# The fifth part of an output projection takes another quarter of x, some sums move earlier, one input load moves later

## The chip, the cores and the metric

The kernel runs on one core of a Trainium2 chip. The metric is the device time of one execution in microseconds (us), lower is better, as the median of several executions. Engines are named as in the profile: PE (matrix multiply), PEld (its weight load), DVE (vector), ACT (activations), POOL (GpSimd), SP (which here only issues transfers).

## What is computed

Eight images of 512 channels by 32x32 pixels (a matrix of 512 by 1024) each go through two attention layers with different weights. In each layer

```python
xn  = group_norm(x, 8 groups) * gamma + beta
q, k, v = wq @ xn + bq, wk @ xn + bk, wv @ xn + bv      # 512 x 1024 each, 8 heads of 64
att = softmax(q_head.T @ k_head / 8)                    # 1024 x 1024 for each head
x   = x + wp @ (att @ v_head for all heads) + bp
```

All numbers are 32-bit floats. The output is x after the second layer.

## The kernel before

**Jobs.** An image in a layer is a job. Images go in pairs, so jobs 0 to 3 are image 0 in layer 0, image 1 in layer 0, image 0 in layer 1, image 1 in layer 1, then the next pair. Image 0 stays in one tile x of 128 partitions by 4 chunks by 1024 columns through jobs 0 and 2.

**One pass of the main loop (variable n)** runs the attention of job n, then the V product of job n+1, and then three projections product by product: O, the output projection of job n, and K and Q of job n+1. The profile shows this as stages: an attention of 110 us and then a stretch of projections of 88 to 94 us.

**Projections by seven products.** Each 512x512 by 512x1024 projection is done by Strassen's scheme in Winograd's form, with 7 half-size products in place of 8, and each of the seven is again done with 7 products of quarter size. The outer seven are called parts here and run in the order `OUTER = (1, 2, 6, 5, 7, 3, 4)`. A part is computed by a chain of seven PE steps (`chain`), in the order 1, 5, 6, 2, 7, 3, 4. The chain's result goes into a tile p of [128, 2, 512] out of the pool `epool`. Chains overlap: step j of chain c stands at place 7c+2j in PE's order, so a step of one chain alternates with a step of the next. After step 7 of a chain DVE reads the PSUM bank that step 4 of the same chain adds to again (`put(1, 1, z)` and then `product(4)` into z). Step 4 therefore waits for DVE.

**How a part reaches x.** `end(c)` runs in program order after the last step of chain c. For the output projection it calls `more(oh, sh, part, moved)`: part is to be added to the quarter (oh, sh) of x, where oh is the half of the channels and sh the half of the columns. With `moved` the sum is made by an accumulating transfer that POOL issues at once (L682). Without it an addition on DVE (L684) goes into the list `outer`, from which `thunk` takes one entry after each step 7 and each step 3 of later chains, and only when the list `soon` is empty. `soon` first holds four sums of the next job's xn and then four sums for the later output chains. The first entry of `outer` is so taken out at chain index 4, after `end(3)`, which is that of part 5. Quarter (0, 0) gets parts 1 and 2, quarter (0, 1) gets 6, 5 and 3, quarter (1, 1) gets 5 and 7, and quarter (1, 0) gets 7 and 4. Part 6 and part 7 are first combined on DVE with parts 1 and 6 (L668).

**DVE and ACT in attention.** For each of 64 steps PE makes a block of scores (L870), ACT its exponentials e (L875), DVE adds e to a running sum (L885 for the first two blocks of a group, L887 for the others) and PE multiplies e by v (L901). e comes from a pool of 6 buffers. After 8 steps `finish` reduces the sum (L917) and takes the product out of PSUM (L924). Between the steps a table of chores places other work at chosen steps. In pass 0 these are factors of weights (L154 to L160), the norm of job 1, the sums of xn for job 1 (`sums`, L385 to L391) and the sums of those sums (`deep_steps`, L423 to L429).

**Orders.** The orders of PE, ACT and DVE are the order in which the code calls them. SP's and POOL's orders come from the layer that builds the program, which also puts in the waits: an instruction that touches the same bytes as an earlier one waits for it. `later(delay, fn)` calls fn once a clock of the program's own, counted in assumed microseconds, has gone that far.

**Input of image 1.** `load_x(1)` issues four transfers of 512 KB on SP during the first projections (L219), into a tile that before held the raw Q weights. ACT reads it at steps 3 to 6 of the first attention.

Of the kernel before, what the change touches and what calls it, by code (L numbers as in the profile page):

```python
# [72 lines left out]
def fast_path(  # L73
# [34 lines left out]
    def later(delay, fn):  # L108
        todo.append((clock[0] + delay, fn))
# [96 lines left out]
    def used(key):  # L206
        del held[key]
        later(2.5, fetch)
# [8 lines left out]
    def load_x(b):  # L217
        for cc in range(NC):
            nc.sync.dma_start(xs[b][:, cc, :], x[b, cc * P : (cc + 1) * P, :])  # L219

    class Norm:
# [20 lines left out]
        def sums(self, cc):  # L242

            nc.scalar.activation(
                xn[0][:, cc, :], xs[self.b][:, cc, :], AF.Identity, accum_out=self.mv[:, cc, 0:1]
            )
# [327 lines left out]
    def deep_phases(n, extra, outs=None, early=()):  # L574
# [8 lines left out]
        def job(which):  # L583
            return n - 1 if which == O else n
# [74 lines left out]
        def end(c):  # L659
            which, o = chains[c]  # L660
            m = job(which)
            used((m, which, o))

            def p(k):
                return tiles[which, k]

            def add(to_, a, b):
                outer.append(lambda: nc.vector.tensor_add(to_, a, b))  # L668

            if which == O:  # L670
                b, layer = jobs[m]
                xt = xs[b]

                def more(oh, sh, part, moved=False):


                    cols = slice(sh * HALF, (sh + 1) * HALF)
                    to_ = xt[:, 2 * oh : 2 * oh + 2, cols]

                    def go():  # L680
                        if moved:
                            nc.gpsimd.dma_start(to_, p(part), accum_op=ALU.add)  # L682
                        else:
                            nc.vector.tensor_add(to_, to_, p(part))  # L684
                        parts[oh, sh] -= 1
                        if layer == 1 and parts[oh, sh] == 0:
                            rows = slice(oh * CH, (oh + 1) * CH)
                            later(8.0 if moved else 2.0, lambda: nc.sync.dma_start(
                                out[b, rows, cols].rearrange("(c p) s -> p c s", p=P), to_
                            ))  # L690

                    if moved:
                        go()
                    else:
                        outer.append(go)

                if o == 1:
                    more(0, 0, 1, True)
                elif o == 2:
                    more(0, 0, 2, True)  # L700
                elif o == 6:
                    add(p(6), p(6), p(1))
                    more(0, 1, 6)
                elif o == 5:
                    more(0, 1, 5)
                    more(1, 1, 5, m in (0, 2))
                elif o == 7:
                    add(p(7), p(7), p(6))
                    more(1, 0, 7)
                    more(1, 1, 7)  # L710
                elif o == 3:
                    more(0, 1, 3, True)
                elif o == 4:
                    more(1, 0, 4, True)
                return
            d = dst[which]

            def quarter(oh, sh):
                return d[:, 2 * oh : 2 * oh + 2, sh * HALF : (sh + 1) * HALF]

            if o == 2:
                add(quarter(0, 0), p(1), p(2))
            elif o == 6:
                add(p(6), p(6), p(1))
            elif o == 5:
                add(quarter(0, 1), p(6), p(5))
            elif o == 7:
                add(p(7), p(7), p(6))
                add(quarter(1, 1), p(7), p(5))
            elif o == 3:  # L730
                add(quarter(0, 1), quarter(0, 1), p(3))
            elif o == 4:
                add(quarter(1, 0), p(7), p(4))
# [28 lines left out]
        at = sorted((7 * c + 2 * j, c, j) for c in range(len(chains)) for j in range(7))  # L762
        at = [(c, j) for _, c, j in at]
# [6 lines left out]
    def last_weights(n):  # L770
        w = acts.tile([P, NW, 2, CH], F32, tag="deep", name="w_last")
        nc.sync.dma_start(w, factors[O, jobs[n][1]])
        return w
# [10 lines left out]
    def last_sums(sh):  # L784


        def start():
            if sh == 0:
                tx[0] = acts.tile([P, 3, 2, HALF], F32, tag="t", name="t_last")
            nc.vector.tensor_sub(last_right(sh, 5), last_right(sh, 7), last_right(sh, 1))  # L790

        def second():
            nc.vector.tensor_sub(last_right(sh, 6), last_right(sh, 3), last_right(sh, 5))

        def third():
            nc.vector.tensor_sub(last_right(sh, 7), last_right(sh, 3), last_right(sh, 7))

        def fourth():
            nc.vector.tensor_sub(last_right(sh, 4), last_right(sh, 2), last_right(sh, 6))

        return start, second, third, fourth
# [258 lines left out]
    def extend_plan(n):  # L1060
        plan.extend((n, V, o) for o in ORDER)
        plan.extend((n - 1, O, o) for o in ORDER)
        plan.extend((n, which, o) for which in (K, Q) for o in OUTER)
# [212 lines left out]
    for n in range(-1, len(jobs)):  # L1276
        last = n + 1 == len(jobs)
        outs = None
        if n >= 0:
            chores = {}  # L1280

            def put(i, fn):
                while i in chores:
                    i += 1
                chores[i] = fn

            if last:
                w = last_weights(n)
                for i, fn in enumerate(last_sums(0)):
                    put(44 + 3 * i, fn)  # L1290
            else:
                if n == 0:
                    first_factors(put, [(O, 0), (V, 1)])
                elif n == 1:
                    first_factors(put, [(K, 1), (Q, 1)])
                elif n == 2:
                    first_factors(put, [(O, 1)])
                for i, (_, fn) in enumerate(extra):
                    put(2 + i, fn)
                at = (10, 19, 22, 24, 26, 28, 36, 39, 42, 45)  # L1300
                if n == 0:
                    for i, fn in zip((3, 3, 4, 5, 6, 8, 10, 11, 12, 13, 15), reads):
                        put(i, fn)
                    at = (22, 30, 34, 35, 37, 38, 41, 44, 47, 50)
                for i, fn in zip(at, steps + sums(n + 1)):
                    put(i, fn)
                deep_first = deep_steps(n + 1)
                for at, fn in zip((52, 54, 57, 59), deep_first[4:]):
                    put(at, fn)
                put(61, lambda: (extend_plan(n + 1), [fetch() for _ in range(RING)]))  # L1310
            assert max(chores, default=0) < NT * len(att.groups)
            att.run(chores)
            banks(0, "one")
            banks(1, "one")
            if last:
                for i, fn in enumerate(last_sums(1)):
                    later(4.1 + 1.5 * i, fn)
                later(9.9, judge)
                for sh in range(2):
                    last_proj(n, w, sh)  # L1320
                break
            outs = OutputSums(n)
            out_sums(n, outs)
            first = v_phase(n + 1, ORDER)
            for thunk in first[:-1]:
                thunk()
            rest = first[-1:]
            extra = deque()
            if jobs[n][1] == 1 and jobs[n][0] + 2 < B:
                extra.append((11, lambda b=jobs[n][0] + 2: (x_tile(b), load_x(b))))  # L1330
            if n == 1:
                load, bias_steps = make_out_bias(1)
                extra.append((8, load))
                extra.extend((11, fn) for fn in bias_steps)
            if n + 2 < len(jobs):
                reads, steps = norm_steps(n + 2)
                extra.extend((15, fn) for fn in reads)
        both = deep_phases(n + 1, extra, outs, deep_first[:4] if outs else ())
        both[0]()
        rest[0]()  # L1340
        if n < 0:
            later(22.0, lambda: load_x(1))
        for thunk in both[1:]:
            thunk()
        banks(0, "two")
        att = Attention(n + 1)
        att.scores(0)
        att.scores(1)
        banks(1, "two")
        att.scores(2, "po")  # L1350
# [249 lines left out]
```

## Time and profile before

| what | value |
|---|---|
| median of three executions | 3208.58 us (3206.6 to 3208.76) |
| the profiled execution's own time | 3205.31 us |
| its span, first to last instruction | 3203.5 us |
| PE busy | 3184.0 us, 99% of the span |
| DVE busy | 2773.0 us, 87% |
| ACT busy | 1913.1 us, 60% |
| POOL busy | 100.7 us, 3% |
| share of 16 DMA engines, SP's and POOL's transfers | 26.5% and 6.2% |

A line of the timeline gives the start in us from the span's beginning, the duration, the engine, the line of the code, the operation, the tile written and those read, how many instructions were merged, and in brackets the engine's idle time before it and what ended it. The chain of waits is the path that ended last, followed back from the end. Times of single instructions are from the profiled execution.

### The profile page before, as it was taken

The numbers are of one execution on the slowest core, as the hardware profiler recorded it, in microseconds if no ns is written. First come the engines' busy times: TensorE is split into PE (matmuls) and PEld (weight loads), VectorE is DVE, ScalarE is ACT, GpSimd is POOL, SyncE is SP. The second block draws the span as 40 slices with busy tenths as digits, with TensorE's granted clock in tenths as the row PEclk, the third lists the DMA queues.
The fourth block names the chain that finished last, engine by engine and source line by source line (L and its number), as shares of the span: only waits on it lengthen the run. The fifth ranks groups of instructions, "written<-read, shape, count | busy, mean of one in ns | idle before, by whom it ended". The sixth has DMA issues, their size and how long they took to land.

```text
span 3203.5 us, 57787 instructions
## 1 busy us (share of the span) xinstructions
PE 3184.0 (99%) x22917; PEld 1861.8 (58%) x22917; DVE 2773.0 (87%) x3989; ACT 1913.1 (60%) x3063; POOL 100.7 (3%) x95
## 2 busy tenths in 40 slices
PE   9999999999999999999999999999999999999999
PEld 7366384663836648366483754837547375573844
DVE  8897999979889798897988889888898888988877
ACT  4746646466565665656656565565656656566564
POOL 0000000000000000000000000000000000000000
PEclk9999999999999999999999999999999999999999
DMA  8234172350703315033160421505216051150511
GB/s 291 74 108 126 49 215 69 94 167 22 213 25 91 88 28 159 21 105 130 30 210 16 119 67 38 147 16 142 96 44 194 16 141 44 51 135 20 170 37 42
DMA packets 156998, 308.32 MB, mean 96 GB/s; under 512 B 34104, under 2 KB 60592, under 8 KB 156464
## 3 DMA queue, kind: packets, MB, share of 16 engines
q1 hardware_dynamic: 139856, 272.05, 26.5%
q0 software_dynamic: 16864, 32.51, 6.2%
q8 instruction: 181, 2.97, 0.4%
q14 instruction: 97, 0.79, 0.1%
HBM read 225.13 MB, written 45.68 MB: 85 GB/s over the span
## 4 chain that ended last, share of the span: by engine, by line
PE 95%; DVE 4%; DMA 0%; issue 0%; POOL 0%; ACT 0%; DVEq 0%; POOLq 0%
PE sc L870 27%; PE po L901 27%; PE zd L636 10%; PE vd L636 10%; PE z L494 6%; PE yd L636 5%; PE ud L636 4%; PE y L494 2%; PE v L494 2%; PE u L494 2%; DVE acc L887 0%; DMA x<-p 0%; PE z_last L814 0%; DVE w L156 0%; DVE p L655 0%
## 5 line engine op out<-in xcount | busy, mean ns | idle before, releaser
L875 ACT ACTIVATE e<-sc 128x1024 f32<-128x1024 f32 x1024 | 1044.3, 1024 | 564.2 <-PE sc L870 458.7
L870 PE MATMUL sc<-q,k 64*64 64x512 f32 x8192 | 1058.2, 589 | 0.0
L901 PE MATMUL po<-e,v 64*64 64x512 f32 x8192 | 1057.3, 589 | 0.0
L887 DVE TENSOR_TENSOR acc<-acc,e 128x1024 f32<-128x1024 f32 x768 | 936.4, 1219 | 58.7 <-ACT e L875 12.0
L901 PEld LDWEIGHTS po<-e,v 64*64 64x64 f32 x8192 | 313.2, 133 | 565.7 <-issue 553.3
L870 PEld LDWEIGHTS sc<-q,k 64*64 64x64 f32 x8192 | 311.5, 133 | 562.4 <-issue 544.8
L885 DVE TENSOR_TENSOR acc<-e,e 128x1024 f32<-128x1024 f32 x128 | 156.4, 1222 | 112.2 <-ACT e L875 112.1
L636 PE MATMUL zd<-deep,w 128*128 128x256 f32 x860 | 241.1, 380 | 2.7 <-DVE p L653 2.1
L636 PE MATMUL vd<-deep,w 128*128 128x256 f32 x804 | 224.3, 380 | 1.4 <-DVE p L655 1.3
L636 PEld LDWEIGHTS zd<-deep,w 128*128 128x128 f32 x860 | 162.8, 190 | 27.2 <-DVE p L653 3.4
L636 PEld LDWEIGHTS vd<-deep,w 128*128 128x128 f32 x804 | 152.3, 190 | 23.9 <-DVE p L655 2.5
L917 DVE TRANSPOSE_TENSOR_REDUCE r<-acc 128x32 f32<-128x1024 f32 x128 | 158.5, 1238 | 0.6
L682 POOL DMA_DIRECT2D x<-p x62 | 74.6, 1211 | 1971.4 <-ACT p L646 1525.1
L636 PE MATMUL vd<-os,w 128*128 128x256 f32 x420 | 118.1, 380 | 1.6 <-DVE p L655 1.6
L668 DVE TENSOR_TENSOR p<-p,p 128x1024 f32<-128x1024 f32 x94 | 114.2, 1215 | 0.0
L494 PE MATMUL z<-w,t 128*128 128x256 f32 x480 | 110.9, 379 | 0.0
L494 PE MATMUL z<-w,xn 128*128 128x256 f32 x480 | 110.1, 382 | 0.0
L518 ACT COPY v<-z 128x512 f32<-128x512 f32 x32 | 18.7, 585 | 148.7 <-PE z L494 148.7
L494 PEld LDWEIGHTS z<-w,xn 128*128 128x128 f32 x480 | 90.0, 190 | 23.8 <-issue 12.2
L442 ACT COPY ud<-zd 128x256 f32<-128x256 f32 x156 | 55.7, 357 | 76.6 <-PE zd L636 75.7
L653 DVE TENSOR_TENSOR p<-vd,s 128x256 f32<-128x256 f32 x63 | 26.7, 424 | 85.1 <-PE vd L636 85.1
L657 ACT COPY s<-vd 128x256 f32<-128x256 f32 x156 | 58.0, 372 | 69.7 <-PE vd L636 69.7
(242 smaller groups left out, 4192.6 us busy)
## 6 DMA issues: line engine op xcount, KB each, us to landing
w<-deep SPq DMA_DIRECT2D x287, 448.0 KB, 3.8
x<-p POOLq DMA_DIRECT2D x62, 512.0 KB, 6.6
rb<-rd SPq DMA_DIRECT2D x96, 256.0 KB, 4.0
w<-keep SPq DMA_DIRECT2D x84, 256.0 KB, 2.7
deep<-w SPq DMA_DIRECT2D x42, 448.0 KB, 3.7
w<-wqkv_dram SPq DMA_DIRECT2D x57, 256.0 KB, 2.8
x<-x_dram SPq DMA_DIRECT2D x28, 512.0 KB, 6.4
out_dram<-x SPq DMA_DIRECT2D x28, 512.0 KB, 6.4
```

Of the source, the lines that this page charges most:

```text
L442: nc.scalar.copy(u, z)
L494: nc.tensor.matmul(ps[:, ti * CH : (ti + 1) * CH], right(src, tx[0], o)[:, cc, t0 : t0 + P], w[:, cc, :], start=(start and ti == 0 and cc ...
L636: nc.tensor.matmul(ps, lhs[:, FACTOR[i], :], moving[i], start=start, stop=True, skip_group_check=True,)
L657: return chain(product, lambda ps: nc.scalar.copy(s5, ps), put, z, y, u, w)
L668: outer.append(lambda: nc.vector.tensor_add(to_, a, b))
L682: nc.gpsimd.dma_start(to_, p(part), accum_op=ALU.add)
L870: nc.tensor.matmul(sc[h * HD : (h + 1) * HD, j, :], k[r, hp, k0 : k0 + HD], q[r, hp, sh * HALF : (sh + 1) * HALF], start=True, stop=True,)
L875: nc.scalar.activation(e, sc, AF.Exp, scale=SCALE)
L885: nc.vector.tensor_add(acc[g], self.es[i - 1], e)
L887: nc.vector.tensor_add(acc[g], acc[g], e)
L901: nc.tensor.matmul(po[g][j * HD : (j + 1) * HD, h, :], v[r, kc, d0 : d0 + HD], e[r, j, :], start=(kc == 0), stop=(kc == NT - 1),)
L917: nc.vector.tensor_reduce(self.r[:, 0, m, :], self.acc.pop(g).rearrange("p j (b e) -> p (j b) e", e=RP), AX.X, ALU.add, apply_transpose=True,)
```

## The change

There are three edits.

1. In the output projections of jobs 0 and 2, the accumulating transfer of part 5 goes to quarter (0, 1), and the addition of part 5 to quarter (1, 1) is now DVE's. Before it was the other way round. In other jobs DVE makes both, before and after.
2. In the first attention (n = 0) the last chores are placed at earlier steps: the four sums of xn at 39, 41, 43, 45 (before 41, 44, 47, 50) and the last four of `deep_steps` at 47, 49, 51, 53 (before 52, 54, 57, 59). The two applications of the norm that were asked for at steps 37 and 38 are asked for at 36 and 37. Since step 35 is taken and a taken step passes a chore on to the next, all four stand where they stood.
3. `load_x(1)` is due 32 of the program's own microseconds after the first projections begin, before 22. In SP's order the first two of the four transfers stay where they were. The third now comes after the fetch of the last Q weights and one store of weight factors, and the fourth after two stores more.

```diff
@@ deep_phases, end(c)
+                fresh = m in (0, 2)
                 if o == 1:
                     more(0, 0, 1, True)
 ...
                 elif o == 5:
-                    more(0, 1, 5)
-                    more(1, 1, 5, m in (0, 2))
+                    more(0, 1, 5, fresh)
+                    more(1, 1, 5)
@@ chores of the attention
                 if n == 0:
 ...
-                    at = (22, 30, 34, 35, 37, 38, 41, 44, 47, 50)
+                    at = (22, 30, 34, 35, 36, 37, 39, 41, 43, 45)
                 for i, fn in zip(at, steps + sums(n + 1)):
                     put(i, fn)
                 deep_first = deep_steps(n + 1)
-                for at, fn in zip((52, 54, 57, 59), deep_first[4:]):
+                for at, fn in zip((47, 49, 51, 53) if n == 0 else (52, 54, 57, 59), deep_first[4:]):
                     put(at, fn)
@@ first projections
         if n < 0:
-            later(22.0, lambda: load_x(1))
+            later(32.0, lambda: load_x(1))
```

## The prediction, made before the changed kernel ran

> **What bounds the kernel now.** I read the page's busy shares first, then PE's waits stage by stage, then DVE, POOL and PE around the waits.
>
> ```profile
> span 3203.5 us, 57787 instructions
> PE 3184.0 (99%) x22917; PEld 1861.8 (58%) x22917; DVE 2773.0 (87%) x3989; ACT 1913.1 (60%) x3063; POOL 100.7 (3%) x95
> ```
>
> PE is busy 99%. Only time in which PE waits can be won; any new wait of PE comes on top. PE's waits in the projections after job 0 (192 to 286 us), then after job 2 (599 to 689 us):
>
> ```profile
> PE zd L636 <- DVE p L653: 2.1, 2, 1.5
> PE v L494 <- DVE q L924: 1.1, 1, 1.1
> PE vd L636 <- DVE p L655: 0.6, 1, 0.6
> ...
> PE zd L636 <- DVE p L653: 0.6, 1, 0.6
> PE vd L636 <- DVE p L655: 0.6, 1, 0.6
> ```
>
> All are for DVE, 5.0 us together, and the list is empty in the attention (82 to 192 us). The longest, 1.5, is where edit 1 acts. In the timeline of that stage DVE takes chains' results between its additions to x (L684):
>
> ```profile
> 236.56 1.21 DVE L684 TENSOR_TENSOR x<-x,p 128x1024 f32<-128x1024 f32 x1
> 237.78 0.48 DVE L655 SCALAR_TENSOR_TENSOR p<-vd,out_step,s 128x256 f32<-128x256 f32 x1
> 238.18 1.22 DVE L684 TENSOR_TENSOR x<-x,p 128x1024 f32<-128x1024 f32 x1
> ...
> 241.37 1.21 DVE L684 TENSOR_TENSOR x<-x,p 128x1024 f32<-128x1024 f32 x1
> 242.51 0.48 DVE L655 SCALAR_TENSOR_TENSOR p<-ud,out_bias,s 128x256 f32<-128x256 f32 x1
> 245.35 1.23 DVE L684 TENSOR_TENSOR x<-x,p 128x1024 f32<-128x1024 f32 x1 [2.37 <-DMA x<-p]
> 246.49 0.42 DVE L653 TENSOR_TENSOR p<-zd,s 128x256 f32<-128x256 f32 x1
> ```
>
> The four L684 are part 6 into (0, 1), part 5 into (0, 1), part 7 into (1, 0), part 7 into (1, 1). The last waits for the transfer of part 5 into (1, 1), and PE waits for the read behind it. The transfer in the chain of waits and PE in the timeline:
>
> ```profile
> 234.81 10.52 DMA x<-p
> ...
> 238.87 0.59 PE L636 MATMUL vd<-os,w 128*128 128x256 f32 x2
> ...
> 246.96 0.70 PE L636 MATMUL zd<-deep,w 128*128 128x256 f32 x2 [1.48 <-DVE p L653]
> ```
>
> So part 5 leaves at 234.81 and lands at 245.32. After job 2 POOL issues it at 638.97, it takes 6.2 to land (645.1), and nobody waits: the addition of part 7 to (1, 1) comes only at 647.33. There:
>
> ```profile
> 638.97 1.20 POOL L682 DMA_DIRECT2D x<-p  x1 [1.33 <-ACT p L646]
> ...
> 641.14 1.22 DVE L684 TENSOR_TENSOR x<-x,p 128x1024 f32<-128x1024 f32 x1
> 642.35 0.48 DVE L655 SCALAR_TENSOR_TENSOR p<-vd,out_step,s 128x256 f32<-128x256 f32 x1
> ```
>
> [...] The trace has 6.2 to 11.1 us in these two stages and decides. [...] Here the granted clock was 0.50 in 9 to 12 us, after a patchy start of PE, and 1.00 in 245 to 248 us around the 1.48 wait. [...] the read at 246.49 ran only behind the addition that waited 2.37.
>
> **Edit 1, part by part.** Work is conserved: DVE still makes four L684 additions of 1.13 us start to start, POOL five transfers. What changes is who waits. In program order part 5's transfer comes before the addition of part 6, which is only taken out of the list `outer` one chain later. Both now touch quarter (0, 1). The changed program's order of instructions with their waits confirms it: in both jobs the addition of part 6 waits for the semaphore of part 5's transfer, and the last L684 waits for no transfer any more. The wait moves forward by three additions.
>
> Behind it in DVE's queue stands the read of chain 5's step 7 (237.78), for which PE's step 4 of that chain (238.87) waits, and PE runs in order. From landing to that step the trace shows 246.96 - 245.32 = 1.64 us with the same pair of DVE operations (an L684 and a read). From there to the last L684 and the read of chain 7, DVE needs five additions and five reads in all from the landing: 5 x 1.13 + 5 x 0.42 = 7.8 us, and PE's fourteen steps of 0.43 between the two points give the same (1.64 + 6.0 = 7.7). So chain 7's step 4, at 246.96 before, stands at landing + 7.8.
>
> After job 0: the landing was at 245.32. It depends on POOL's issue at 234.81, after ACT's and DVE's last write of part 5, which nothing moves. PE's stall holds back one weight fetch (issued at 239.50 before, behind step 4) that shared the engines at the end; I take 0.5 us for it, landing 244.8 (estimate; bounds 243.6 and 245.3). Then 244.8 + 7.8 - 246.96 = **+5.6** (4.4 to 6.1). The 1.48 that is removed is already inside.
>
> After job 2: landing 645.12, for which DVE waits from 641.14, 4.0 us. Chain 5's step 4 ran at 643.45 and chain 7's fourteen steps later, at 649.5. Now 645.12 + 7.8 - 649.5 = **+3.4** (3.0 to 4.5).
>
> Clock: PE stands from about 239.4 to 246.4 after job 0, 7.0 us[...]; after job 2 from 643.6 to 646.8, 3.2 us[...]. The start shows one such half-rate window. Half rate for one window costs 3.4 / 2 = 1.7 us; none costs 0; two cost 3.4. I take one after job 0 (1.7) and 0.7 after job 2, where it may not come. **+2.4** (0 to 5).
>
> **Edit 2.** It can only help if DVE is done sooner when PE leaves the attention. The end of it:
>
> ```profile
> 187.83 2.55 DVE L887 TENSOR_TENSOR acc<-acc,e 128x1024 f32<-128x1024 f32 x2
> 190.30 0.95 DVE L429 TENSOR_TENSOR deep<-t,deep 128x768 f32<-128x768 f32 x1
> 191.17 5.21 DVE L887 TENSOR_TENSOR acc<-acc,e 128x1024 f32<-128x1024 f32 x4
> 196.41 1.25 DVE L917 TRANSPOSE_TENSOR_REDUCE r<-acc 128x32 f32<-128x1024 f32 x1
> 197.58 0.65 DVE L924 TENSOR_TENSOR q<-po,px 128x512 f32<-128x512 f32 x1
> ```
>
> DVE has no idle time from 120.4 on to 234 us; it runs from its queue. The eight moved sums (four of 1.13, four of 0.87) leave the end and enter between 153 and 182 us, where DVE is full too. The sum to the last L924 is the same, so the 1.07 of PE's wait for it stays. Cost in between: additions of e come later, by up to 3.1 us, and ACT needs an e buffer back after six. By summing durations in the new order from 153.40 (the first order change), the tightest is the addition of block 54, done at 183.05, for the exponential that started at 184.18: 1.1 us left. The gather of L944 lands 3.1 us after its L917 (170.7 to 173.8), so at 175.5 in the new order, for a use at 177.1. **0**, bounds -0.5 and +2: additions to one sum back to back take 1.27 to 1.33 each against 1.13 with other work between, and a few pairs change; a late gather would stall DVE for up to the 1.9 that it does once before (at 120.4).
>
> **Edit 3.** No PE wait in 0 to 82 us is for a transfer, so nothing is to be won. The last of the four moves from 61.5 behind a store at 72.8 and lands by 80.6 with the slowest of its transfers (7.3 us); ACT needs it at 94.71. Cover 14 us. **0**.
>
> Sum: 5.6 + 3.4 + 2.4 = 11.4 us. The profiled execution's own time, 3205.31, would be 3216.7. The runs' median is 3.3 above it; 3208.58 + 11.4 = **3220.0**.
>
> **Rivals.** What a measurement of this kernel can tell from no change is about 0.2%, 6.4 us.
>
> (a) *The wait is shorter than worked out.* POOL's transfers vary; with landings 5.4 us after issue (the shortest of later stages, if queueing behind part 2 allowed it) and no loss of clock, the two come to 240.2 + 7.8 - 246.96 = +1.0 and 644.4 + 7.8 - 649.5 = +2.7: 3212.3. Against it: after job 0 part 2's transfer, issued just ahead, itself lands only at 240.9.
>
> (b) *Not slower.* If part 5 lands before DVE reaches part 6's addition, the move is pure gain: the 1.48 and some 0.3 around 241.8 vanish, -1.8 us, and with the sums sooner at most the other waits of that stage, 1.1 + 0.6 + 0.6: 3204.5. It decides where the transfer takes under 236.56 - 234.81 = 1.75 us after job 0 and 2.2 us after job 2; no transfer of this kind is that quick.
>
> (c) *The transfers land late.* At the 11.1 us of the slowest one after job 2, with two half-rate windows at each stall: 6.1 + 8.4 + 5 = +19.5, 3228.
>
> (d) *No effect.* Edits 2 and 3 alone: 0. For edit 1 it would need DVE or PE to have slack behind part 6; PE's step 4 stands 1.1 us behind the read, no more.
>
> **Chances.** The worked case, +6.5 to +15: 0.83. (a) 0.08, (b) 0.02, (c) 0.05, (d) 0.02. Slower by over 0.2%: 0.83 + 0.05 = 0.88; within: (a), (d) and the part of (b) near zero, 0.11; faster 0.01. The range, +5 to +17 us, leaves out most of (b), (c), (d) and half of (a): 3213.5 to 3225.5.
>
> **What would show it.** After the change the first L684 after job 0 and after job 2 should show idle time ended by "DMA x<-p", about 8 and 4 us; the fourth none. PE should have two waits for L655 of about 7.0 and 3.2 us in place of the 1.48. The granted clock should dip after the first. PE's wait for L924 should still be about 1.1. It is wrong if part 6's addition starts without waiting, if the V product's wait disappears (then DVE was not full), or if ACT waits for L887 in the first attention.

## The result and the profile after

| | before | after |
|---|---|---|
| median of six executions each | 3207.82 us | 3219.61 us |
| ratio, 95% interval | | 1.0039 (1.0029 to 1.0048) |
| span of the profiled execution | 3203.5 us | 3217.5 us |
| projections after job 0, from their first product to the next scores | 93.81 us | 101.96 us |
| projections after job 2, the same | 89.72 us | 96.02 us |

The change costs 11.8 us, 0.39%. The six executions of the kernel before are the three given above and three more. In the two profiled executions the stretches after jobs 0 and 2 grew by 8.15 and 6.30 us. All other stretches agree within 0.05 us but the last, which is 0.45 us shorter.

From line 694 on, line numbers are one higher in the changed kernel, so that its L925 is the L924 of before. Its page begins:

```profile
span 3217.5 us, 57792 instructions
PE 3188.8 (99%) x22916; PEld 1864.0 (58%) x22917; DVE 2772.8 (86%) x3989; ACT 1915.0 (60%) x3063; POOL 100.7 (3%) x95
```

DVE and POOL do as much work as before. PE is busy for 4.8 us more with the same number of products, less one record: some of them ran slower. What PE waited for in the two stretches, first after job 0 and then after job 2 (who, for what, us in total, times, longest):

```profile
PE vd L636 <- DVE p L655: 8.3, 2, 7.6
PE v L494 <- DVE q L925: 1.4, 1, 1.4
PE zd L636 <- DVE p L653: 0.6, 1, 0.6
...
PE vd L636 <- DVE p L655: 3.7, 2, 3.1
PE zd L636 <- DVE p L653: 0.6, 1, 0.6
```

The 1.5 us after job 0 is gone, and waits of 7.6 and 3.1 us stand in its place. DVE's timeline shows where they start, again first after job 0:

```profile
236.54 0.42 DVE L653 TENSOR_TENSOR p<-ud,s 128x256 f32<-128x256 f32 x1
245.29 1.23 DVE L684 TENSOR_TENSOR x<-x,p 128x1024 f32<-128x1024 f32 x1 [8.33 <-DMA x<-p]
246.43 0.48 DVE L655 SCALAR_TENSOR_TENSOR p<-vd,out_step,s 128x256 f32<-128x256 f32 x1
...
252.72 1.21 DVE L684 TENSOR_TENSOR x<-x,p 128x1024 f32<-128x1024 f32 x1
...
653.11 1.22 DVE L684 TENSOR_TENSOR x<-x,p 128x1024 f32<-128x1024 f32 x1 [3.80 <-DMA x<-p]
654.25 0.48 DVE L655 SCALAR_TENSOR_TENSOR p<-vd,out_step,s 128x256 f32<-128x256 f32 x1
```

The wait for the transfer has moved from the fourth L684, which now has no wait (252.72), to the first, that of part 6, and after job 2 there is one where none was. PE's timeline behind the first wait, and the first line behind the second:

```profile
246.97 1.22 PE L636 MATMUL vd<-os,w 128*128 128x256 f32 x2 [7.62 <-DVE p L655]
247.98 1.06 PE L636 MATMUL yd<-to,w 128*128 128x256 f32 x2
248.84 1.06 PE L636 MATMUL zd<-xn,w 128*128 128x256 f32 x2
...
251.31 0.59 PE L636 MATMUL ud<-to,w 128*128 128x256 f32 x2
251.74 0.59 PE L636 MATMUL zd<-deep,w 128*128 128x256 f32 x2
...
654.78 1.22 PE L636 MATMUL vd<-os,w 128*128 128x256 f32 x2 [3.08 <-DVE p L655]
```

Up to 251 us the steps follow each other every 0.85 us and not every 0.43. The table of stretches (start and end, length, busy time of PE, PEld, DVE, ACT and POOL, granted PE clock, DMA share, GB/s) has the reason in its third last column:

```profile
243.70:252.00 8.30, 5.03 (x14) 4.12 (x15) 5.49 (x7) 1.68 (x4) 1.20 (x1) 0.59 0.38 91
653.70:662.00 8.30, 7.22 (x20) 5.89 (x21) 6.92 (x9) 2.54 (x7) 1.20 (x1) 0.59 0.98 270
3000.00:3010.00 10.00, 10.00 (x48) 8.81 (x47) 9.53 (x20) 1.22 (x3) 0.00 (x0) 1.00 0.46 138
```

The records of the granted clock have 0.50 from 244.38 to 251.21 and from 653.98 to 660.81 us, 6.83 us each and twice the 3.41 us of the one such window in the first 20 us. PE worked in 4.2 and 6.0 us of them, so by this estimate about 2.1 and 3.0 us went to the clock.

### The profile page after: what moved, and what is told of

It reads as the page before. It is cut to its first block, busy times and chain, and to the rows that moved or that the text cites. A ratio compares the mean times of both kernels' runs of the same rounds, so it can differ in the third digit from the quotient of the medians.

```text
span 3217.5 us, 57792 instructions
## 1 busy us (share of the span) xinstructions
PE 3188.8 (99%) x22916; PEld 1864.0 (58%) x22917; DVE 2772.8 (86%) x3989; ACT 1915.0 (60%) x3063; POOL 100.7 (3%) x95
## 4 chain that ended last, share of the span: by engine, by line
PE 79%; DVE 1%; DMA 0%; issue 0%; ACT 0%; DVEq 0%
PE sc L871 22%; PE po L902 22%; PE zd L636 9%; PE vd L636 9%; PE z L494 5%; PE yd L636 4%; PE ud L636 4%; PE v L494 1%; PE u L494 1%; PE y L494 1%; PE z_last L815 0%; DVE acc L888 0%; DMA x<-p 0%; DVE q L979 0%; DVE x L837 0%
## 5 line engine op out<-in xcount | busy, mean ns | idle before, releaser
L636 PE MATMUL zd<-deep,w 128*128 128x256 f32 x860 | 241.2, 380 | 1.1 <-DVE p L653 0.6
L636 PE MATMUL vd<-deep,w 128*128 128x256 f32 x804 | 225.1, 381 | 1.4 <-DVE p L655 1.3
L636 PEld LDWEIGHTS zd<-deep,w 128*128 128x128 f32 x860 | 163.4, 190 | 24.8 <-DVE p L653 1.5
L636 PEld LDWEIGHTS vd<-deep,w 128*128 128x128 f32 x804 | 152.9, 191 | 24.2 <-DVE p L655 2.5
L636 PE MATMUL vd<-os,w 128*128 128x256 f32 x420 | 119.4, 383 | 12.3 <-DVE p L655 12.2
L657 ACT COPY s<-vd 128x256 f32<-128x256 f32 x156 | 58.2, 373 | 72.0 <-PE vd L636 72.0
```

The lines of the kernel that those rows point to most:

```text
L636: nc.tensor.matmul(ps, lhs[:, FACTOR[i], :], moving[i], start=start, stop=True, skip_group_check=True,)
L657: return chain(product, lambda ps: nc.scalar.copy(s5, ps), put, z, y, u, w)
```

## The experiments

The theory was that of the prediction: part 5's transfer stands ahead of part 6's addition in program order, DVE waits for its landing, and PE waits behind DVE and then runs at half clock for a while. The rivals were that edits 2 and 3 bear part of the loss, that a transfer into that quarter is slow wherever it stands, and that the slow stretch behind the wait is DVE's and not PE's clock. Unless said otherwise an edit is to the changed kernel, and a stretch is named by its job.

### Edit 1 alone, and edits 2 and 3 alone

```diff
 # edit1: the kernel before with
-                    more(0, 1, 5)
-                    more(1, 1, 5, m in (0, 2))
+                    more(0, 1, 5, m in (0, 2))
+                    more(1, 1, 5)
 # edits23: the changed kernel with
-                    more(0, 1, 5, fresh)
-                    more(1, 1, 5)
+                    more(0, 1, 5)
+                    more(1, 1, 5, m in (0, 2))
```

> The kernel before with edit 1 alone (part 5's transfer to the second quarter), edits 2 and 3 left out. Theory of the prediction: the whole loss is edit 1's, so this is 11 to 13 us slower than before, the projections after job 0 last about 102 us (93.8 before) and those after job 2 about 96 us (89.7 before), each with one PE wait for L655 of about 7.5 and 3 us. Rival: edits 2 and 3 bear part of the loss (in the changed kernel DVE leaves the first attention 0.3 us later than before); then this is at least 1 us less slow than the changed kernel.

> The changed kernel with edit 1 undone: sums sooner in the first attention and the second input later. Theory: DVE is full from 120 to 234 us, so where its work stands in there changes nothing: same as before within 1 us, the last L924 (a line number later here) again at about 197.6 and PE's wait for it again 1.1 to 1.4 us. Rival: sums sooner free DVE at the end of the attention; then the wait of 1.1 us goes and the waits of 0.6 behind it too, up to 2.3 us faster.

Edit 1 alone: 3218.91 against 3206.62 us, ratio 1.0038 (1.0024 to 1.0051), stretches of 102.12 and 94.80 us. Edits 2 and 3 alone: 3206.28 us, 0.9999 (0.9991 to 1.0007). The loss is edit 1's. In the run without it DVE ends the first attention as in the kernel before, to 0.05 us:

```profile
197.63 0.65 DVE L925 TENSOR_TENSOR q<-po,px 128x512 f32<-128x512 f32 x1
```

It was 197.58 before. PE's wait for it is 0.9 to 1.4 us in the profiles with edit 2, and 0.9 (edit 1 alone) and 1.1 (before) in the two without. So moving the sums inside a stretch in which DVE is never idle gained nothing. Edit 3 was not run without edit 2, so 0.9999 is the two together.

### The new quarter in job 0 alone

```diff
-                    more(0, 1, 5, fresh)
-                    more(1, 1, 5)
+                    more(0, 1, 5, m == 0)
+                    more(1, 1, 5, m == 2)
```

> The changed kernel with the new quarter in job 0 alone; in job 2 part 5's transfer goes to the last quarter as before. Theory: the two losses are independent. Projections after job 0 about 102 us as in the changed kernel, those after job 2 back at 89.7 us with no DVE wait for a transfer; the whole about 8 us slower than before. Rival: the wait after job 2 follows from the lateness of job 0; then it stays in part, above 92 us.

One execution: 3213.1 us beside a median of 3206.86 before. The stretches are 101.73 and 90.20 us, and after job 2 DVE waits for no transfer. So the loss after job 2 does not follow from that of job 0. (The new quarter in job 2 alone was not run.) The total, 6.2 us above, is less than the 8.4 of the stretches (7.9 + 0.5); one execution can't tell the difference.

### The waiting addition placed later

```diff
                 elif o == 6:
                     add(p(6), p(6), p(1))
-                    more(0, 1, 6)
+                    if not fresh:
+                        more(0, 1, 6)
                 elif o == 5:
                     more(0, 1, 5, fresh)
                     more(1, 1, 5)
+                    if fresh:
+                        more(0, 1, 6)
```

> The changed kernel with DVE's additions of part 6 to (0, 1) and of part 5 to (1, 1) exchanged in jobs 0 and 2: the addition that waits stands one addition and one chain's read later. Theory (the wait lasts until the transfer lands, and PE waits only for reads behind it): the landing is where it was, DVE's wait is shorter by 1.6 us (about 6.7 and 2.2), PE loses 1.7 us less in each stage, and after job 2 PE's clock may not be halved any more (3 us): 3.4 to 6.5 us less slow than the changed kernel. Rival: the loss comes from the transfer's own time on the DMA engines, not from its place in DVE's order; then the time is that of the changed kernel within 1 us.

3215.3 us, ratio 1.0026 (1.0016 to 1.0036): 8.4 us above the kernel before, 3.4 less than the changed kernel's 11.8. But the gain came from one stretch alone, 91.50 us after job 2 (96.02 in the changed kernel), while that after job 0 stayed at 102.11. What PE waited for in that stretch:

```profile
PE zd L636 <- DVE p L655: 6.5, 1, 6.5
```

PE's timeline behind that wait:

```profile
249.72 1.22 PE L636 MATMUL zd<-os,w 128*128 128x256 f32 x2 [6.53 <-DVE p L655]
250.74 1.06 PE L636 MATMUL yd<-xn,w 128*128 128x256 f32 x2
```

The wait is 1.1 us shorter (7.62 to 6.53), in the direction expected. The clock ate it: it stayed at 0.50 from 245.68 to 255.92 us, 10.24 and not 6.83, of which 6.2 us held work. After job 2 PE waited for 1.5 us and the clock stayed at 1.00. So the place of the addition counts, against the rival. But the length of the wait alone does not set the time at half rate: behind waits of 7.62 us it was 6.83 us in the changed kernel and 10.24 with edit 1 alone, and here 10.24 behind 6.53 (the records are laid out below, in the part on the clock).

### PE kept busy during the wait

Products whose output nobody reads, ahead of the step of chain 5 that has to wait. This is an addition to the kernel's work:

```diff
-            z, y, u, w = (bank(half, b, f"{b}d_{n}_{c}")[:, :QT] for b in names)
+            z, y, u, w = (bank(half, b, f"{b}d_{n}_{c}") for b in names)
+            spare[c] = z[:, QT:]
+            z, y, u, w = (t[:, :QT] for t in (z, y, u, w))
...
+        spare = {}
...
+                if outs and c == 5 and j == 6:
+                    for _ in range({0: 32, 2: 12}.get(n - 1, 0)):
+                        nc.tensor.matmul(
+                            spare[c], env.blk, env.blk.unsqueeze(1).to_broadcast([P, 2, P]),
+                            start=False, stop=True, skip_group_check=True,
+                        )
```

> The changed kernel with idle products of 128x256 put into PE's queue right before the step that waits: 32 in job 0 and 12 in job 2 (some 0.22 us each, 6.9 and 2.6 us, less than the waits of 7.6 and 3.1 us), into an unused half of a PSUM bank; they change no result. Theory: part of the loss is PE's clock, granted at half for 6.8 us behind each wait, of which 4.2 and 6.0 us held work, so 2.1 and 3.0 us lost. Kept busy, PE keeps its clock: granted clock 1.00 throughout, 4 to 5 us less slow than the changed kernel, with projections after job 0 about 99.9 us and after job 2 about 93.0 us. Rival: the slow stretch behind the wait is DVE working off its queue, not PE's clock; then nothing changes, or it is slower by what the products overshoot.

This run did not test the theory: it took 3239.25 us. Its products wrote a bank whose other half DVE had still to read, so the first of them waited with everything behind it, the profile naming DVE for 7.3 us. The clock fell as before (its mean was 0.997, that of the changed kernel's profiled execution), and the products then came on top. So whether they would have kept the clock up stayed open here. One product of 128x256 also proved to be two records of 0.22 us, 0.43 in all. Mended, with a bank that nobody had still to read, and half as many:

```diff
-            spare[c] = z[:, QT:]
+            spare[c] = w[:, QT:]
...
-                    for _ in range({0: 32, 2: 12}.get(n - 1, 0)):
+                    for _ in range({0: 16, 2: 6}.get(n - 1, 0)):
```

> The idle products of the run fill again, mended: they now write the unused half of the bank that the chain's second step used, which nobody reads any more, so that they need not wait for DVE themselves; and half as many, 16 in job 0 and 6 in job 2, since one product of 128x256 turned out to take 0.43 us of PE: 6.9 and 2.6 us. Theory: PE's granted clock stays at 1.00 behind the waits, the projections after job 0 last about 99.9 us (101.96 in the changed kernel) and those after job 2 about 93.0 us (96.02), the whole 4 to 5 us less slow than the changed kernel. Rival: what is slow behind the wait is DVE working off its queue; then both stages stay within 0.5 us of the changed kernel's.

3214.78 us, ratio 1.0023 (1.0014 to 1.0033), 7.6 us above the kernel before and 4.2 less than the changed kernel. PE's timeline around the step that waits (L749 holds the products nobody reads; the lines for the steps and DVE's reads, L638 and L657, are L636 and L655 of the changed kernel):

```profile
238.97 7.07 PE L749 MATMUL zd<-blk 128*128 128x256 f32 x32
246.87 0.70 PE L638 MATMUL vd<-os,w 128*128 128x256 f32 x2 [0.83 <-DVE p L657]
247.40 0.59 PE L638 MATMUL yd<-to,w 128*128 128x256 f32 x2
247.83 0.59 PE L638 MATMUL zd<-xn,w 128*128 128x256 f32 x2
```

The table of stretches for the same time, the clock again third from the end:

```profile
236.00:250.00 14.00, 13.17 (x62) 11.17 (x60) 5.55 (x9) 3.92 (x10) 1.11 (x1) 1.00 0.69 165
```

DVE waits for the transfer as long as before (8.4 us), PE's step comes at the same distance, but the steps behind it are 0.43 us apart at once and the clock is 1.00 throughout. The stretches are 99.68 and 93.86 us, 2.3 and 2.2 less than in the changed kernel, although after job 2 the transfer landed late here (DVE waited 4.5 us, not 3.8). This shows the half clock to be a loss of its own behind the wait, and not DVE working off its queue. It also gives the size of the wait without it: 99.68 - 93.81 = 5.9 us after job 0, 93.86 - 89.72 = 4.1 after job 2, of which 0.7 is that late landing.

### The transfer behind part 6's addition

```diff
-                    more(0, 1, 5, fresh)
+                    if fresh:
+                        sixth = outer.pop()
+                        outer.append(lambda: (sixth(), more(0, 1, 5, True)))
+                    else:
+                        more(0, 1, 5)
                     more(1, 1, 5)
```

> The changed kernel, but in jobs 0 and 2 part 5's transfer is issued in program order just behind DVE's addition of part 6 to the same quarter, so that the transfer waits for DVE and not DVE for the transfer. Theory: the loss is the wait that program order puts in front of part 6's addition. With it gone no L684 waits for a transfer: projections after job 0 about 92 us (1.5 to 2 less than the kernel before), after job 2 about 89.7 as before, the whole 1 to 2 us faster than before. Rival: a transfer into that quarter is bad in itself, since part 3's transfer into the same quarter and those behind it in POOL's queue come later; then some 5 us or more of the loss stay.

3208.28 us, 1.0004 (0.9995 to 1.0012): the loss is gone, the gain did not come. After job 0 the stretch is 92.63 us, as expected. After job 2 it is 92.33, 2.6 above the kernel before, and the waits of PE there name something new:

```profile
PE vd L636 <- DMA w<-deep: 2.1, 1, 2.1
```

There the transfer lands at 652.5, part 3's into the same quarter is issued behind it at 653.1, and SP's store of that quarter to the output, for which job 2 is the last layer, waits until 660.0. SP's queue behind the store holds weights. This is read from the order of SP's queue; in the last run below, in which job 2 keeps the last quarter, PE has no such wait. So the rival had a point: not the loss of the changed kernel, but a smaller one hangs on how late part 3's transfer is.

### No transfer of part 5

```diff
-                fresh = m in (0, 2)
+                fresh = False
```

> The changed kernel with no transfer of part 5 at all: DVE makes both additions in jobs 0 and 2, one addition of 1.13 us more in each. Theory: without the transfer nothing waits; DVE's extra 1.13 us after job 0 costs less than the 2.37 that it waited in the kernel before: projections after job 0 about 92.5 us, after job 2 up to 0.5 above the 89.7 of before, the whole within 0 to 1.5 us faster than before. Rival: DVE is the bound in these stretches, and its extra additions come out in full, 1.1 us in each, 1 to 2 us slower than before.

3204.39 us, 0.9992 (0.9984 to 1.0001), stretches of 93.06 and 89.70 us. DVE's extra addition costs nothing after job 2 and less than the wait that it replaces after job 0. That is 0.8 us in the stretches; the interval reaches no change.

### The pieces that gained, together

```diff
-                    more(0, 1, 5, fresh)
-                    more(1, 1, 5)
+                    if m == 0:
+                        sixth = outer.pop()
+                        outer.append(lambda: (sixth(), more(0, 1, 5, True)))
+                        more(1, 1, 5)
+                    else:
+                        more(0, 1, 5)
+                        more(1, 1, 5, m == 2)
```

> The changed kernel with the new quarter in job 0 alone, and there with part 5's transfer issued behind DVE's addition of part 6 (as in behind6); in job 2 part 5's transfer goes to the last quarter as in the kernel before. Theory: the loss of behind6 after job 2 came from its outputs, which wait for the late transfers in SP's queue and hold up weights; job 0 has no outputs. So projections after job 0 about 92.6 us (93.8 before) and after job 2 about 89.7 us (92.3 in behind6), the whole 1 to 1.5 us faster than before, about what 5 rounds can tell. Rival: the lateness of transfers in job 0 costs elsewhere later; then no stage sum shows the 1.2 us.

3205.11 us against 3207.14, 0.9993 (0.9985 to 1.0002): not told apart from the kernel before. After job 2 the stretch is 89.74 us, as expected. After job 0 it is 93.57, not 92.6. PE's and DVE's waits there:

```profile
PE zd L636 <- ACT yd L438: 1.4, 1, 1.4
...
DVE p L655 <- DMA x<-p: 1.4, 1, 1.4
```

Part 2's transfer still reads a buffer that a later chain needs, and ACT and DVE wait for it (2.3 and 1.4 us). In the kernel before ACT waited 0.98 us for it under the cover of DVE's own lateness. With that lateness gone this wait is the next to reach PE, and by how much varies (0.9 us in the run with both transfers moved, with the same code in job 0).

## Why the prediction was right

**The time.** Forecast +11.4 us and 3220.0; measured +11.8 and 3219.61. That the total is so close is in part luck. In the profiled pair the loss is 13.95 us (3205.31 and 3219.26), for the clock cost twice what was put down for it. And the median before of these six executions, 3207.82, is high: 68 later ones, in three groups, had medians of 3206.62 to 3207.14, and against them the loss is 12.5 to 13.0.

**Edit 1's wait.** The step "DVE's wait moves forward by three additions, PE's step stands 1.64 us behind the landing" held: landing 245.20 (taken 244.8), step at 246.97, 1.77 behind. The waits of DVE, put at about 8 and 4 us, were 8.33 and 3.80; PE's, put at 7.0 and 3.2, were 7.62 and 3.08. The sums, +5.6 and +3.4, answer to +5.9 with the clock kept up, and to 6.30 - 3.0 = +3.3 after job 2 by subtracting the clock's share. The issue, which nothing was to move, came at 235.14 and not 234.81, and the transfer took 10.06 us and not 10.52. Whether a held-back weight fetch gave it that half microsecond is not plain: it took 10.0 to 10.4 us in four profiles with this stall and 10.5 and 10.9 in the two without edit 1, but 10.6 with PE kept busy, where the step came as late.

**The clock.** The dip came, and its size was off. The term was +1.7 after job 0 and +0.7 after job 2; measured are 2.1 to 2.3 and 2.2 to 3.0. The dip was expected after the first wait and came after both, and the term's upper bound, 5, was about reached. What the kernel before shows behind the term is one record of 0.50 near the start, from 8.68 to 12.09 us, 3.41 us long, of which half was charged. That a stall of PE would bring such a stretch, and one alone, was the author's estimate: around the 1.48 us wait the clock was 1.00.

All records of the granted clock in the two kernels' profiles but the last of each, at the end of the program, last one or more times 3.413 us (in the changed kernel the full clock stood for 232.11 us and for 402.77 us between half-rate stretches, 68 and 118 times that). These steps are called windows here. Behind the waits the half rate stood for one to three windows, and it ended with the first window that PE worked through (in one case all but 0.27 us of it). Laid over PE's waits, the records give

| stretch | PE idle in the window before the half rate, us | PE idle in the windows at half rate, us |
|---|---|---|
| changed kernel, after job 0 | 3.41 | 2.59, then 0.00 |
| changed kernel, after job 2 | 2.28 | 0.80, then 0.00 |
| edit 1 alone, after job 0 | 3.09 | 3.41, then 1.12, then 0.00 |
| edit 1 alone, after job 2 | 3.03 | 0.27 |
| addition placed later, after job 0 | 2.71 | 3.41, then 0.63, then 0.00 |

The new quarter in job 0 alone fits in: its PE came back at 246.68 after 7.73 us, with steps every 0.85 us until about 251 and every 0.43 from there. The windows did not begin with PE's return: in the changed kernel the half rate began at 244.38 and PE came back at 246.97. The rest of the window in which PE came back ran at half rate as well, and then one more whole window, but none after the rest that was nearly all of one (0.27 idle). That is what the term left out: from PE's return to the end of the half rate are 4.2 and 6.0 us of work, not 3.4 and some part of it. In the changed kernel after job 0 a window with 1.62 us idle (237.56 to 240.97) was followed by the full clock; those of the table's second column, with 2.28 us idle and more, were followed by half. Near the start of the program the half rate followed windows with 1.14 us idle (the kernel before) and 1.15 (the changed one), so the two numbers hold for these stretches alone.

Executions differ in this share. The mean granted clock is on record for all six of the changed kernel: from 0.999 in the fastest (3217.38 us) through 0.998 (3219.02) and 0.997 (3219.26, the profiled one, to 3220.86) to 0.996 in the slowest (3221.60). Where the others ran at half clock is not shown, since only one has a profile.

**Edits 2 and 3.** Put at 0, measured 0.9999. The reason given, DVE full in the whole stretch, was shown by its end at 197.6 in both orders. The changed kernel's own end is 197.91: there DVE waited 2.3 and not 1.9 us for a gather at about 120 us, ahead of the first moved sum. With the same two edits and no edit 1 that wait was 1.9 us and the end 197.63. The delay of additions that was feared for ACT did not come: its waits in the first attention come to 29.6 us, 29.7 before. One reading was off without effect: the last of the four input transfers stands at 68.86 and not behind the store at 72.8.

**The rivals.** No transfer of part 5 landed early, and none took 11.1 us, the longest of the 62 that POOL issued in the kernel before (5.4 us at the shortest, 6.6 in the median). Rival (c) had a sum that doesn't follow from its terms: two windows at each stall are 6.8 us at its own price and not 5, and after job 0 it took the landing at 245.3 and not 11.1 us after issue. Two windows at each stall did come in the profiled execution, but PE stood idle in part of them, so they cost about 5. That the wait could be had for nothing in another order was not among the rivals; the runs show that it can, and how little it is worth.

## What to carry to other kernels

When two writers share a buffer, look at which comes first in program order: here DVE's addition waited 8.33 us for the transfer ahead of it, and not at all with the transfer behind it. Before moving an accumulating transfer to another target, list in the new order which instructions on the target stand behind it, and ask how much work of the same engine is queued behind the first of them. A stall of PE of a few microseconds is to be priced with the clock that was granted behind it: here the waits of 7.62 and 3.08 us were followed by 4.2 and 6.0 us of work at 0.50, by the estimate above 2.1 and 3.0 us lost. And moving work about inside a stretch where its engine was never idle gained nothing here (0.9999).

## What the runs showed that was not expected

The first projections, the same code in most of these runs, took 80.09 to 81.80 us in the profiled executions. The two longest, 81.80 and 81.48, are those with two half-clock windows in a row near the start (6.83 us); those with one recorded (3.41 us) took 80.09 to 80.52. In the three others (80.68 to 80.81) the records begin only at 10.2 to 13.0 us. What stands ahead of the first record is taken here as half rate, by the time of the products: a pair of 128x512 took 2.06 us at 6.84 in one of these (the addition placed later); in the kernel before, whose records begin at 5.27, it took 2.07 us at 1.49, and 1.10 us at 6.42 with a clock of 1.00. Counted so from the start of the span, the half rate lasted for 8.6 to 9.4 us in the runs with one window recorded, 10.2 to 13.0 in these three and 11.3 to 11.4 in the longest two; only the one with 13.0 us, that without part 5's transfer (80.81), is out of order. A difference of over a microsecond between two executions of this kernel can so lie in its first stage alone.
